# Graph net on one core: the scaling product issued behind the finished block, the column stored behind the rows, index work ahead of the degree counts

## The chip, the core and the metric

The kernel runs on one core of one Trainium2 chip. TensorE (PE) does the matrix products, VectorE (DVE) and ScalarE (ACT) the element-wise work, GpSimd (POOL) issues the indirect DMAs that gather rows, and SyncE (SP) issues the other DMAs. The metric is the device time of the program in microseconds; the time of a kernel is the median of several executions.

## What is computed

`x` has 6250 rows (nodes) of 512 float32; `src` and `dst` are 100000 edges, sorted by `dst`. Cut to what matters, the reference is:

```python
def _cheb_norm(src, dst, n):
    deg = segment_sum(ones, src, num_segments=n)
    dinv = where(deg > 0, rsqrt(maximum(deg, 1.0)), 0.0)
    return -dinv[src] * dinv[dst]

def _cheb_conv(x, src, dst, norm, W0, W1, b):
    tx1 = segment_sum(x[src] * norm[:, None], dst, num_segments=n)
    return x @ W0 + tx1 @ W1 + b

h = maximum(layernorm(x), 0.0)
h = _cheb_conv(h, src, dst, norm, W1_0, W1_1, b1)
h = _layer_norm(h, gamma, beta)
h = where(h >= 0, h, 0.01 * h)
return x + _cheb_conv(h, src, dst, norm, W2_0, W2_1, b2)
```

Each of the two layers gathers one row of 512 floats for every edge, sums the gathered rows by target node, and multiplies rows and sums by two 512 x 512 matrices.

## The kernel before, in words

**Tiling.** Nodes are cut into 49 blocks of 128 (`NB`), edges into 782 chunks of 128 (`NC`). One indirect DMA of POOL gathers one chunk, 128 rows, into one slot of the ring `places` (55 slots, `R`). Three chunks are a unit, four units a group; there are 66 groups (`NS`). Group 0 holds chunks 0 to 2, group 1 chunks 3 to 14, and so on by twelves; group 4 is chunks 39 to 50, group 64 759 to 770, and the last, group 65, 771 to 781. Gather number n writes slot n modulo 55, so that gather 94 overwrites chunk 39, the first of group 4.

**Tables.** Layer 0 gathers from `tab[0]`: rows of relu(layernorm(x)), whose column 512 holds the node's `dinv`. Layer 1 gathers from `tab[1]`, rows of the first layer's output, already scaled. While `tab[0]` is being made, the first 64 chunks (`RAW`) are gathered from `x` itself (`gather_raw`, L232 to L234) and scaled afterwards, when `look_up` (L475 to L495) has found the factors of their rows: it makes one-hot products on PE (L469, L484), multiplies them on DVE (L472, L487, L490, L493) and lets ACT scale four slots (L495). Its tile `both` (L489) lies in the buffer named `g`, of which there is one; `finish` uses that buffer too.

**Prologue.** `x` comes into the ring by blocks. DVE and PE count the degrees with one-hot matrices (L284 to L314; `lo` and `hi` at L300, 25 turns, into which ACT's row statistics and the row stores L272 are mixed). `load_rest` (L193) loads the rest of `x`, then, at its numbers 3 and 4, the two weights of the first layer and four bias rows. Behind the counts come `dinv`, the column store L340 (column 512 of the first 31 blocks of `tab[0]`, each piece four bytes), the last blocks' rows, and the index work L356 to L389: target indices transposed (L368, L371, L372), the units' first nodes (L375, L376), `node_of` (L388).

**The loop over groups** (L768 on) does for each group g: `gather_to` (issue the gathers up to a ring ahead), in layer 0 `look_up`, then `turn` for each block that is due (all its groups have been summed): `place` (L620 to L630: DVE's comparison `there` L628 and PE's product L630 bring the unit sums to the block's rows), and `own` (L507 to L516, the block's own rows turned by PE). Then `choose` (L549, the selection matrices `sel`), in layer 0 `scale` (L588 to L598: DVE multiplies `sel` by the gathered column 512, so it waits for the gathers of the group), `sums` (L601 to L618: PE's product L609 of `sel` and gathered rows), and `dense` for the due blocks (L684 to L698: PE's transposes L688, DVE's copy L690, 16 PE products L526), which calls `finish`. `finish` (L633 to L669) adds the bias (L647), takes the statistics (L650, L651), normalizes (L655 to L657), makes the scaled row (L660, L661), stores it to `tab[1]` (L664), makes the unscaled row in `g` (L666, L667) and stores it to `h_tab` (L669).

**The layer boundary.** For blocks 46 to 48 the part with the block's own rows is made early (`EARLY`, `early` L537). At group 64 the due blocks' `dense` comes ahead of the sums, and `gather_ahead` (L444 to L447) issues 18 gathers of layer 1, which need only the rows of `tab[1]` up to block 46; the next gathers (L437) need all of them.

**What sets the order.** On PE, POOL and SP instructions go in the order in which the code issues them (`manual_schedule`; in the prologue on SP alone). On DVE and ACT a scheduler puts them in order; `issue_after` gives it an instruction behind which another must be placed. Each engine works through its order one by one, and a waiting instruction holds what stands behind it.

Of the kernel before, what the change touches and what calls it, by code (L numbers as in the profile page):

```python
# [8 lines left out]
F32 = mybir.dt.float32  # L9
# [32 lines left out]
def gnn_kernel(  # L42
# [194 lines left out]

    gather_raw(0, RE)


    rs_all, nb_all = ln[:, 0, :], ln[:, 1, :]
    nm_all = ep.tile([P, NB], F32, name="nm_all")
# [41 lines left out]
    with tc.tile_pool(name="deg", bufs=1) as dp, tc.tile_pool(name="onehot", bufs=2) as ohp, tc.tile_pool(  # L284
        name="deg_ps", bufs=1, space=bass.MemoryType.PSUM
    ) as dps:
        s_lo = dp.tile([EP, EJ], BF, name="s_lo")
        s_hi = dp.tile([EP, EJ], BF, name="s_hi")
        half_i = dp.tile([EP, EJ], I32, name="half_i")
        nc.vector.tensor_single_scalar(half_i, src_i, LO - 1, op=OP.bitwise_and)  # L290
        nc.vector.tensor_copy(s_lo, half_i)
        half_i = dp.tile([EP, EJ], I32, name="half_i")
        nc.vector.tensor_single_scalar(half_i, src_i, 6, op=OP.arith_shift_right)
        nc.vector.tensor_copy(s_hi, half_i)
        both_ps = dps.tile([P, 2 * HI], F32, name="both_ps")
        for g in range(EJ // (2 * GJ)):
            hot = []
            for s, n, name in ((s_lo, LO, "lo"), (s_hi, HI, "hi")):
                t = ohp.tile([EP, GJ, n, 2], BF, name=name)
                nc.vector.tensor_tensor(  # L300
                    t, s[:, g * 2 * GJ : (g + 1) * 2 * GJ].rearrange("p (j s) -> p j s", s=2)[:, :, None, :]
                    .to_broadcast([EP, GJ, n, 2]),
                    iota_g[:EP, None, :n, :].to_broadcast([EP, GJ, n, 2]), op=OP.is_equal)
                hot.append(t.rearrange("p j n s -> p j (n s)"))
            k = turns.get(g)
            if k is not None:
                spread(*some[k])
                make_table(*some[k])
                load_rest(k - 1)
                if k + 2 < len(some):  # L310
                    stats(*some[k + 2])
            for j in range(GJ):
                nc.tensor.matmul(both_ps, hot[0][:, j, :], hot[1][:, j, :], start=(g == 0 and j == 0),
                                 stop=(g == EJ // (2 * GJ) - 1 and j == GJ - 1))  # L314
        nc.vector.tensor_copy(both, both_ps.rearrange("p (b t s) -> p b t s", t=2, s=2))
# [20 lines left out]
        nc.vector.tensor_scalar_mul(ndinv, dinv, -1.0)  # L336
        nc.vector.tensor_scalar_mul(sdinv, dinv, SLOPE)

    early = NB - LAST
    nc.sync.dma_start(tab[0][: early * P, D : D + 1].rearrange("(i p) o -> p i o", p=P), dinv[:, :early, None])  # L340
    for i0, n in others:
        cols = slice(i0, i0 + n)
        st = ep.tile([P, 7, 6], F32, name="st")
        mv = ep.tile([P, 7, 2], F32, name="mv")
        for j in range(n):
            nc.vector.bn_stats(st[:, j, :], places[:, RE + i0 + j, :D])
            nc.vector.bn_aggr(mv[:, j, :], st[:, j, :])
        nc.scalar.activation(rs_all[:, cols], mv[:, :n, 1], AF.Sqrt, bias=eps)
        nc.vector.reciprocal(rs_all[:, cols], rs_all[:, cols])
        nc.vector.scalar_tensor_tensor(nb_all[:, cols], mv[:, :n, 0], -1.0, rs_all[:, cols], op0=OP.mult, op1=OP.mult)  # L350
        nc.vector.tensor_copy(places[:, RE + i0 : RE + i0 + n, D : D + 1], dinv[:, cols, None])
        make_table(i0, n)
    nc.vector.tensor_mul(sc[:, 0, :], rs_all, dinv)
    nc.vector.tensor_mul(sc[:, 1, :], nb_all, dinv)

    low = ep.tile([P, P], I32, name="low")  # L356
    nc.vector.tensor_single_scalar(low, chunks[0][:, 0, :], P - 1, op=OP.bitwise_and)
    nc.vector.tensor_copy(src_lo, low)
    nc.vector.tensor_copy(pick, ident)


    nc.vector.memset(dlx[:, 0:1], 0.0)
    nc.vector.memset(dlx[:, 1 + NC :], float(N))
    with tc.tile_pool(name="turn", bufs=1) as wp, tc.tile_pool(
        name="turn_ps", bufs=1, space=bass.MemoryType.PSUM
    ) as wps:
        f = wp.tile([P, NG, P], F32, name="f")
        nc.vector.tensor_scalar_add(f, chunks[1], 1.0)  # L368
        dl_ps = wps.tile([P, NG * P], F32, name="dl_ps")
        for g in range(NG):  # L370
            nc.tensor.transpose(dl_ps[:, g * P : (g + 1) * P], f[:, g, :], ident)  # L371
        nc.scalar.activation(dlx[:, 1 : 1 + NC], dl_ps[:, :NC], AF.Copy)  # L372
        last = ident[:, P - 1 : P]
        first_ps = nodes_ps[:, : NQ * NS + 1]
        nc.tensor.matmul(first_ps, last.to_broadcast([P, P]), dlx[:, 0 : STEP * NQ * NS + 1 : STEP], start=True, stop=True)  # L375
        nc.vector.tensor_copy(first, first_ps)  # L376
        row_ps = wps.tile([P, NS], F32, name="row_ps")
        for q in range(NQ):
            for g, n in ((0, 1), (1, NS - 1)):
                at = STEP * (unit[g] + q)  # L380
                nc.tensor.matmul(row_ps[q * Q : (q + 1) * Q, g : g + n], last.to_broadcast([P, Q]),
                                 dlx[:, at : at + STEP * NQ * (n - 1) + 1 : STEP * NQ], start=True, stop=True)
        p_i = ep.tile([P, 1], I32, name="p_i")
        p_j = ep.tile([P, 1], F32, name="p_j")
        nc.vector.tensor_copy(p_i, p_id)
        nc.vector.tensor_single_scalar(p_i, p_i, Q - 1, op=OP.bitwise_and)
        nc.vector.tensor_copy(p_j, p_i)
        nc.vector.tensor_scalar(node_of, row_ps, p_j, None, op0=OP.add)  # L388
        nc.vector.tensor_scalar_mul(minus, last, -1.0)  # L389

    edges.close()
    unseen = const.tile([1, 1], I32, name="unseen")
# [9 lines left out]
def usual_path(tc, have):  # L402
    nc = tc.nc
    (x, out, tab, h_tab, ndinv, sidx, dlx, iota_r, w_sb, W2_1, W2_0, w_late, ident, eps, ones, first, nodes_ps, node_of, minus,
     unsorted, ln, dinv, sdinv, bias1, bias2, gam, bet, unseen, unit, N, E, D, NB, NC, NU, NS, KD, rows, places, R,
     sc, pick, src_lo, src_hi, eidx, e_src, zero_row, p_id) = (
        have[n] for n in ("x out tab h_tab ndinv sidx dlx iota_r w_sb W2_1 W2_0 w_late ident eps ones first nodes_ps node_of "
                          "minus unsorted ln dinv sdinv bias1 bias2 gam bet unseen unit N E D NB NC NU NS KD rows places "
                          "R sc pick src_lo src_hi eidx e_src zero_row p_id").split())
# [11 lines left out]
    with ExitStack() as es:  # L421
        pool = es.enter_context(tc.tile_pool(name="main", bufs=2))
        psum = es.enter_context(tc.tile_pool(name="main_ps", bufs=2, space=bass.MemoryType.PSUM))
        es.enter_context(tc.manual_schedule(engines={PE, POOL, SP}))
        is_lo, found, looked, gathered = [], 0, 0, R
        own_h, own_x, agg, placed, started, pre, late = {}, {}, {}, {}, {}, {}, {}
        SHIFTED = D - D % P
        lidx = pool.tile([P, NC - SHIFTED], I32, name="lidx", bufs=1)
# [46 lines left out]
        def look_up(tag):  # L475
# [7 lines left out]
            for j in range(4):  # L483
# [2 lines left out]
            is_hi = pool.tile([P, KD, P], F32, name="aT", bufs=1)[:, :, :NB]  # L486
            nc.vector.tensor_tensor(is_hi, src_hi[:, at : at + 4, None].to_broadcast([P, 4, NB]),  # L487
                                    iota_r[:, None, :NB].to_broadcast([P, 4, NB]), op=OP.is_equal)
            both = pool.tile([P, D], F32, name="g", bufs=1)[:, : 8 * NB].rearrange("p (j k b) -> p j k b", j=4, k=2)  # L489
            nc.vector.tensor_tensor(both, at_lo[:, :, : 2 * NB].rearrange("p j (k b) -> p j k b", k=2),  # L490
                                    is_hi[:, :, None, :].to_broadcast([P, 4, 2, NB]), op=OP.mult)
            ac = pool.tile([P, 4, 2], F32, name="ac", bufs=4)
# [127 lines left out]
        def place(i, some):  # L620
# [4 lines left out]
            for g in some:  # L625
                m = Q * (unit[g + 1] - unit[g])
                there = pool.tile([P, P], F32, name="there", bufs=3)
                nc.vector.tensor_scalar(there[:m, :r], iota_r[:m, :r], node_of[:m, g : g + 1], -(1.0 + i * P),  # L628
                                        op0=OP.subtract, op1=OP.is_equal)
                nc.tensor.matmul(placed[i][:r], there[:m, :r], agg[g][:m, :], start=(g == inside[i][0]),  # L630
                                 stop=(g == inside[i][-1]))

        def finish(layer, i, v):  # L633
# [23 lines left out]
            nc.vector.scalar_tensor_tensor(v, v, rs[:r], bet[:r], op0=OP.mult, op1=OP.add)  # L657

            t = late[i] if i in late else pool.tile([P, D], F32, name="t")
            nc.scalar.activation(t[:r], v, AF.Copy, scale=sdinv[:r, i : i + 1])  # L660
# [3 lines left out]
                nc.sync.dma_start(tab[1][at + lo : at + hi, :], t[lo:hi])  # L664
# [81 lines left out]
        high = pool.tile([P, RAW], I32, name="high", bufs=1)  # L746
        nc.vector.tensor_single_scalar(high, sidx[:, :RAW], 7, op=OP.arith_shift_right)
        nc.vector.tensor_copy(src_hi, high)
        find("ps")
        find("ps")  # L750
        for i in range(AHEAD):
            load(0, i)
        for k in range(2):
            look_up("u_ps")
            find("ps")

        for layer in range(2):
# [5 lines left out]
            for g in range(NS):  # L763
# [380 lines left out]
```

## Time and profile before

| quantity | value |
|---|---|
| median of 3 runs | 2081.95 us |
| fastest and slowest run | 2077.32 and 2086.94 us |
| profiled execution, its own time | 2079.41 us |
| span of the profile | 2077.0 us |
| PE, DVE, ACT, POOL busy | 81%, 34%, 21%, 73% of the span |

The profile is of one execution. Its span runs from the first to the last recorded instruction; what lies between span and time is outside the record. A busy share is a mean over the whole span, so the places where an engine waits have to be looked for one by one. PE's matrix products of float32 are recorded in two passes each: x24 stands for 12 products. In the timeline a row gives start, duration, engine, line, the operation's tiles, and in brackets the idle time ahead of it and what ended it. In the chain of waits each row is a step of the chain that ended last. Where a window is shown, the columns are the busy times of PE, weight load, DVE, ACT and POOL with their counts, the granted PE clock as a share, the DMA share and GB/s.

### The profile page before, as it was taken

How to read it: one execution, taken by the hardware profiler on the slowest of the kernel's cores; microseconds unless marked ns; L12 is line 12 of the kernel's file. 1: busy time of each engine (PE TensorE's matmuls, PEld its weight loads, DVE VectorE, ACT ScalarE, POOL GpSimd, SP SyncE). 2: the span in 40 equal slices, each digit the busy share in tenths (PEclk: the TensorE clock that was granted, in tenths of full speed). 3: DMA queues.
4: the chain of work that ended last, by engine and by line, in shares of the span. 5: the costliest groups of instructions: out<-in, count | busy, mean ns of one | idle time of the engine just before them, and what ended most of it. 6: DMA issues, size and time to landing. Idle time of an engine off the chain costs nothing.

```text
span 2077.0 us, 19822 instructions
## 1 busy us (share of the span) xinstructions
PE 1680.6 (81%) x6806; PEld 677.0 (33%) x6806; DVE 696.7 (34%) x1496; ACT 442.0 (21%) x789; POOL 1509.3 (73%) x1578
## 2 busy tenths in 40 slices
PE   4577977886869398779789888898888878888987
PEld 4443432332323143223333323233323223332332
DVE  7964433333344254324353121221212112111221
ACT  8883212222212122222121010110101011010110
POOL 5756777777777777777747777777777777777773
PEclk9778989999879799989999899999999999999999
DMA  9997888888888888888857788887888788888874
GB/s 334 375 288 220 271 262 247 263 261 246 262 281 266 231 277 262 249 263 255 259 171 239 244 247 249 255 256 241 255 240 255 240 256 255 250 246 251 274 237 145
DMA packets 189982, 528.49 MB, mean 254 GB/s; under 512 B 34610, under 2 KB 36172, under 8 KB 189872
## 3 DMA queue, kind: packets, MB, share of 16 engines
q0 software_dynamic: 125120, 415.98, 67.3%
q1 hardware_dynamic: 64752, 111.16, 14.8%
q8 instruction: 55, 0.90, 0.2%
q14 instruction: 55, 0.45, 0.1%
HBM read 475.35 MB, written 51.66 MB: 254 GB/s over the span
## 4 chain that ended last, share of the span: by engine, by line
PE 32%; DMA 29%; POOL 16%; issue 14%; DVE 7%; ACT 2%; DVEq 0%; POOLq 0%; SPq 0%; ACTq 0%
DMA places<-tab,sidx 22%; POOL places L437 16%; PE u_ps L526 13%; PE ps L609 8%; PE an_ps L630 6%; DMA places<-tab,lidx 6%; PE hT_ps L688 1%; DVE lo L300 1%; DVE hi L300 1%; PE hT_ps L514 1%; ACT an L681 1%; PE hT_ps L484 1%; DVE st L650 1%; PE hT_ps L581 0%; DVE sel L598 0%
## 5 line engine op out<-in xcount | busy, mean ns | idle before, releaser
L437 POOL DMA_INDIRECT places<-tab,sidx x1212 | 1149.7, 949 | 376.5 <-issue 268.5
L609 PE MATMUL ps<-places,sel 128*32 128x512 f32 x3128 | 495.6, 642 | 126.5 <-DMA places<-tab,sidx 86.4
L437 POOL DMA_INDIRECT places<-tab,lidx x270 | 255.6, 947 | 82.3 <-issue 63.1
L630 PE MATMUL an_ps<-agg,there 128*128 128x512 f32 (+1 forms) x580 | 277.1, 611 | 17.4 <-ACT agg L618 17.4
L609 PEld LDWEIGHTS ps<-places,sel 128*32 128x32 f32 x3128 | 100.6, 113 | 489.3 <-issue 195.3
L526 PE MATMUL u_ps<-w,aT 128*128 128x512 f32 (+1 forms) x392 | 181.3, 606 | 33.7 <-DVE aT L690 33.7
L565 DVE TENSOR_TENSOR sel<-dlx,nodes_ps 128x384 f32<-128x384 f32 (+3 forms) x134 | 72.1, 539 | 403.3 <-PE ps L609 403.3
L526 PE MATMUL u_ps<-w,hT 128*128 128x512 f32 (+1 forms) x392 | 197.6, 652 | 5.4 <-ACT hT L516 5.4
L618 ACT ACTIVATE agg<-ps 128x512 f32<-128x512 f32 (+1 forms) x132 | 78.5, 594 | 538.5 <-PE ps L609 516.9
L526 PE MATMUL u_ps<-places,hT 128*128 128x512 f32 (+1 forms) x392 | 185.0, 616 | 2.2 <-ACT hT L516 2.2
L526 PE MATMUL u_ps<-places,aT 128*128 128x512 f32 (+1 forms) x392 | 178.2, 598 | 2.3 <-DVE aT L690 2.3
L598 DVE TENSOR_TENSOR sel<-sel,places 128x384 f32<-128x384 f32 (+11 forms) x73 | 35.3, 486 | 380.5 <-DMA places<-tab,sidx 359.4
L688 PE MATMUL hT_ps<-ident,an 128*128 128x128 f32 x392 | 71.8, 311 | 106.0 <-ACT an L681 105.4
L630 PEld LDWEIGHTS an_ps<-agg,there 128*128 128x128 f32 (+1 forms) x580 | 104.8, 196 | 120.9 <-issue 90.3
L641 DVE TENSOR_TENSOR u_ps<-u_ps,bias 128x512 f32<-128x512 f32 x46 | 32.2, 700 | 283.0 <-PE u_ps L526 283.0
L516 ACT ACTIVATE hT<-hT_ps 128x512 f32<-128x512 f32 (+1 forms) x98 | 58.0, 592 | 291.8 <-PE hT_ps L514 291.0
L526 PEld LDWEIGHTS u_ps<-w,aT 128*128 128x128 f32 (+1 forms) x392 | 74.0, 193 | 134.0 <-issue 85.9
L234 POOL DMA_INDIRECT places<-in_x_dram,sidx x55 | 74.9, 1361 | 54.7 <-DMA tab<-places 15.5
L628 DVE TENSOR_SCALAR there<-iota_r,node_of 128x128 f32<-128x128 f32 (+1 forms) x290 | 86.3, 301 | 83.0 <-PE an_ps L630 82.7
L688 PEld LDWEIGHTS hT_ps<-ident,an 128*128 128x128 f32 x392 | 46.1, 154 | 197.6 <-ACT an L681 139.0
L526 PEld LDWEIGHTS u_ps<-w,hT 128*128 128x128 f32 (+1 forms) x392 | 79.3, 213 | 89.8 <-issue 83.7
L526 PEld LDWEIGHTS u_ps<-places,aT 128*128 128x128 f32 (+1 forms) x392 | 74.6, 191 | 96.5 <-issue 93.6
(159 smaller groups left out, 1265.3 us busy)
## 6 DMA issues: line engine op xcount, KB each, us to landing
places<-tab,sidx POOLq DMA_INDIRECT x1212, 3.8
h_tab<-g SPq DMA_DIRECT2D x48, 256.0 KB
xt<-in_x_dram SPq DMA_DIRECT2D x48, 256.0 KB
out_dram<-t SPq DMA_DIRECT2D x48, 256.0 KB
tab<-t SPq DMA_DIRECT2D x47, 256.0 KB
h<-in_x_dram SPq DMA_DIRECT2D x46, 256.0 KB
h<-h_tab SPq DMA_DIRECT2D x46, 256.0 KB
tab<-places SPq DMA_DIRECT2D x22, 528.0 KB
```

Of the source, the lines that this page charges most:

```text
L234: nc.gpsimd.indirect_dma_start(out=places[:, t, :D], out_offset=None, in_=x, in_offset=bass.IndirectOffsetOnAxis(ap=sidx[:, t : t + 1], ax ...
L300: nc.vector.tensor_tensor(t, s[:, g * 2 * GJ : (g + 1) * 2 * GJ].rearrange("p (j s) -> p j s", s=2)[:, :, None, :] .to_broadcast([EP, GJ, ...
L437: nc.gpsimd.indirect_dma_start(out=places[:, t % R, :] if own_scale else zr(layer, t), out_offset=None, in_=x if layer == 0 and t < RAW el ...
L516: nc.scalar.activation(hT[:, :, :r], ps[:, :, :r], AF.Copy)
L526: nc.tensor.matmul(u_ps[:r], hT[:, kc, :r], w[:, kc, :], start=(start and kc == 0), stop=(stop and kc == KD - 1))
L565: nc.vector.tensor_tensor(sel[:, q : q + k, :w, :], of, node[:, q : q + k, None, :].to_broadcast([P, k, w, Q]), op=OP.is_equal)
L598: nc.vector.tensor_tensor(v, v, places[:, lo % R : lo % R + hi - lo, D : D + 1].to_broadcast([P, hi - lo, Q]), op=OP.mult)
L609: nc.tensor.matmul(ps[q * Q : (q + 1) * Q, :], sel[:, q, s, :], zr(layer, chunk[q][s]), start=(s == 0), stop=(s == len(chunk[q]) - 1 and ( ...
L618: nc.scalar.activation(agg[g][: n * Q], ps[: n * Q], AF.Copy)
L628: nc.vector.tensor_scalar(there[:m, :r], iota_r[:m, :r], node_of[:m, g : g + 1], -(1.0 + i * P), op0=OP.subtract, op1=OP.is_equal)
L630: nc.tensor.matmul(placed[i][:r], there[:m, :r], agg[g][:m, :], start=(g == inside[i][0]), stop=(g == inside[i][-1]))
L688: nc.tensor.transpose(ps[:, kc, :r], an[:r, kc * P : (kc + 1) * P], ident[:r, :r])
```

## The change

Three stretches of code change their place, one tile its buffer, and one product its place in DVE's order. No operation is added or left out.

1. The index work (L356 to L389) and the high bits of the source indices (`high`, `src_hi`, L746 to L748) are written ahead of the row statistics and the degree counts.
2. The column store L340 stands behind the row stores of the last blocks instead of ahead of them.
3. The weights and biases (`load_rest(3)`, `load_rest(4)`) are loaded behind the first two loads of `usual_path` instead of in turns of the degree counts.
4. The tile `both` of `look_up` lies in the buffers named `an` (two) instead of `g` (one).
5. In layer 0 `scale` is issued behind the last comparison `there` and behind the last finished block: behind its L657, and from block 45 on behind its last step L667.

```diff
+        high = ep.tile([P, RAW], I32, name="high")
+        nc.vector.tensor_single_scalar(high, sidx[:, :RAW], 7, op=OP.arith_shift_right)
+        nc.vector.tensor_copy(src_hi, high)
...
-                load_rest(k - 1)
+                if k < 4:
+                    load_rest(k - 1)
...
-    early = NB - LAST
-    nc.sync.dma_start(tab[0][: early * P, D : D + 1].rearrange("(i p) o -> p i o", p=P), dinv[:, :early, None])
     for i0, n in others:
...
         make_table(i0, n)
+    early = NB - LAST
+    nc.sync.dma_start(tab[0][: early * P, D : D + 1].rearrange("(i p) o -> p i o", p=P), dinv[:, :early, None])
...
+        behind = {}
...
-            both = pool.tile([P, D], F32, name="g", bufs=1)[:, : 8 * NB].rearrange("p (j k b) -> p j k b", j=4, k=2)
+            both = pool.tile([P, D], F32, name="an")[:, : 8 * NB].rearrange("p (j k b) -> p j k b", j=4, k=2)
...
-                nc.vector.tensor_scalar(there[:m, :r], iota_r[:m, :r], node_of[:m, g : g + 1], -(1.0 + i * P),
-                                        op0=OP.subtract, op1=OP.is_equal)
+                behind[1] = nc.vector.tensor_scalar(there[:m, :r], iota_r[:m, :r], node_of[:m, g : g + 1],
+                                                    -(1.0 + i * P), op0=OP.subtract, op1=OP.is_equal)
...
-            nc.vector.scalar_tensor_tensor(v, v, rs[:r], bet[:r], op0=OP.mult, op1=OP.add)
+            behind[0] = nc.vector.scalar_tensor_tensor(v, v, rs[:r], bet[:r], op0=OP.mult, op1=OP.add)
...
-            nc.vector.tensor_tensor(g[:r], v, g[:r], op=OP.max)
+            end = nc.vector.tensor_tensor(g[:r], v, g[:r], op=OP.max)
+            if i >= NB - 4:
+                behind[0] = end
...
         for i in range(AHEAD):
             load(0, i)
+        load_rest(3)
+        load_rest(4)
...
                 if layer == 0:
-                    scale(sel, chunk)
+                    with ExitStack() as order:
+                        for ins in behind.values():
+                            order.enter_context(tc.issue_after(ins.ins))
+                        scale(sel, chunk)
```

The stretch of the index work is written word for word as it was, only further up.

More of the change, by code (lines that the diff above doesn't have):

```diff
@@ L238, in gnn_kernel @@
     gather_raw(0, RE)
+    low = ep.tile([P, P], I32, name="low")
+    nc.vector.tensor_single_scalar(low, chunks[0][:, 0, :], P - 1, op=OP.bitwise_and)
+    nc.vector.tensor_copy(src_lo, low)
+    nc.vector.tensor_copy(pick, ident)
+    nc.vector.memset(dlx[:, 0:1], 0.0)
+    nc.vector.memset(dlx[:, 1 + NC :], float(N))
+    with tc.tile_pool(name="turn", bufs=1) as wp, tc.tile_pool(
+        name="turn_ps", bufs=1, space=bass.MemoryType.PSUM
+    ) as wps:
+        f = wp.tile([P, NG, P], F32, name="f")
+        nc.vector.tensor_scalar_add(f, chunks[1], 1.0)
+        dl_ps = wps.tile([P, NG * P], F32, name="dl_ps")
+        for g in range(NG):
+            nc.tensor.transpose(dl_ps[:, g * P : (g + 1) * P], f[:, g, :], ident)
+        nc.scalar.activation(dlx[:, 1 : 1 + NC], dl_ps[:, :NC], AF.Copy)
+        last = ident[:, P - 1 : P]
+        first_ps = nodes_ps[:, : NQ * NS + 1]
+        nc.tensor.matmul(first_ps, last.to_broadcast([P, P]), dlx[:, 0 : STEP * NQ * NS + 1 : STEP], start=True, stop=True)
+        nc.vector.tensor_copy(first, first_ps)
+        row_ps = wps.tile([P, NS], F32, name="row_ps")
+        for q in range(NQ):
+            for g, n in ((0, 1), (1, NS - 1)):
+                at = STEP * (unit[g] + q)
+                nc.tensor.matmul(row_ps[q * Q : (q + 1) * Q, g : g + n], last.to_broadcast([P, Q]),
+                                 dlx[:, at : at + STEP * NQ * (n - 1) + 1 : STEP * NQ], start=True, stop=True)
+        p_i = ep.tile([P, 1], I32, name="p_i")
+        p_j = ep.tile([P, 1], F32, name="p_j")
+        nc.vector.tensor_copy(p_i, p_id)
+        nc.vector.tensor_single_scalar(p_i, p_i, Q - 1, op=OP.bitwise_and)
+        nc.vector.tensor_copy(p_j, p_i)
+        nc.vector.tensor_scalar(node_of, row_ps, p_j, None, op0=OP.add)
+        nc.vector.tensor_scalar_mul(minus, last, -1.0)
+        high = ep.tile([P, RAW], I32, name="high")
+        nc.vector.tensor_single_scalar(high, sidx[:, :RAW], 7, op=OP.arith_shift_right)
+        nc.vector.tensor_copy(src_hi, high)
     rs_all, nb_all = ln[:, 0, :], ln[:, 1, :]
@@ L352, in gnn_kernel @@
         make_table(i0, n)
+    early = NB - LAST
+    nc.sync.dma_start(tab[0][: early * P, D : D + 1].rearrange("(i p) o -> p i o", p=P), dinv[:, :early, None])
     nc.vector.tensor_mul(sc[:, 0, :], rs_all, dinv)
     nc.vector.tensor_mul(sc[:, 1, :], nb_all, dinv)
[L356 to L389, printed above, removed]
     edges.close()
@@ L405, in usual_path @@
      unsorted, ln, dinv, sdinv, bias1, bias2, gam, bet, unseen, unit, N, E, D, NB, NC, NU, NS, KD, rows, places, R,
-     sc, pick, src_lo, src_hi, eidx, e_src, zero_row, p_id) = (
+     load_rest, sc, pick, src_lo, src_hi, eidx, e_src, zero_row, p_id) = (
         have[n] for n in ("x out tab h_tab ndinv sidx dlx iota_r w_sb W2_1 W2_0 w_late ident eps ones first nodes_ps node_of "
                           "minus unsorted ln dinv sdinv bias1 bias2 gam bet unseen unit N E D NB NC NU NS KD rows places "
-                          "R sc pick src_lo src_hi eidx e_src zero_row p_id").split())
+                          "R load_rest sc pick src_lo src_hi eidx e_src zero_row p_id").split())
     AHEAD = 2
@@ L744, in check @@
             nc.vector.tensor_single_scalar(unseen, ok[:, 0:1], 0.0, op=OP.is_gt)
-        high = pool.tile([P, RAW], I32, name="high", bufs=1)
-        nc.vector.tensor_single_scalar(high, sidx[:, :RAW], 7, op=OP.arith_shift_right)
-        nc.vector.tensor_copy(src_hi, high)
         find("ps")
```

## The prediction

> **What bounds the kernel now.** I read the page first, then the waits of POOL, then POOL's timeline. The page names the costliest group: the single-chunk gathers.
>
> ```profile
> span 2077.0 us, 19822 instructions
> L437 POOL DMA_INDIRECT places<-tab,sidx x1212 | 1149.7, 949 | 376.5 <-issue 268.5
> ...
> POOL places L437 <- issue: 331.8, 1089, 0.3
> POOL places L234 <- DMA tab<-places: 15.5, 4, 7.5
> ```
>
> A gather takes 0.95 and is followed by 0.30 of issue: 1.25 us each, 15.0 for a group of 12. Beside these pauses of 0.3 the waits (engine and line, who was waited for, us in total, times, longest) hold only a few long ones, and the timeline (start, duration, in brackets the idle time ahead and what ended it) gives their places.
>
> ```profile
> 121.58 0.95 POOL L234 DMA_INDIRECT places<-in_x_dram,sidx  x1 [7.96 <-ACT agg L618]
> ...
> 145.34 0.94 POOL L437 DMA_INDIRECT places<-tab,sidx  x1 [0.30 <-DMA places<-in_x_dram,sidx]
> 187.04 0.94 POOL L437 DMA_INDIRECT places<-tab,sidx  x1 [4.50 <-ACT places L495]
> 1049.23 0.95 POOL L437 DMA_INDIRECT places<-tab,sidx  x1 [0.30 <-issue]
> 1070.53 0.94 POOL L447 DMA_INDIRECT places<-tab,eidx  x1 [20.35 <-DMA tab<-t]
> 1096.05 0.94 POOL L437 DMA_INDIRECT places<-tab,sidx  x1 [3.29 <-DMA tab<-pre]
> ```
>
> From 187.04 to 1049.23 POOL issues without a gap (gathers 94 to 781: 862.2 / 687 = 1.255 each), and again from 1096.05 on. So three things set the time: when gather 94 goes, how long POOL stands between 1049.23 and 1096.05, and a fixed rest. An edit that shortens PE or DVE anywhere else buys nothing. Faster and slower mean by more than 0.5% here, 10.4 us, about what a measurement of this kernel can tell from no change.
>
> **Gather 94: the `both` tile.** Gather 94 overwrites slot 39, the first chunk of group 4, so it waits for that group's products. What held these is in the chain of waits:
>
> ```profile
> 167.67 0.70 DVE u_ps L647
> 168.37 0.26 DVE aT L487
> ...
> 170.87 0.77 DVE u_ps L657
> ...
> 174.52 5.46 DMA h_tab<-g
> 180.07 0.58 DVE g L490
> 181.81 3.52 PE an_ps L630 x6
> 185.32 2.71 PE ps L609 x24
> ...
> 196.40 2.71 PE ps L609 x24
> ```
>
> The look-up at L490 writes into the one buffer `g`, which the first finished block has filled and its store of 256 KB is still reading: 5.46 us, behind L667 of that block. In `an`, with two buffers, neither stands in the way. The earliest L490 can go is behind its operand L487, at 168.6 (gain 11.4); the latest, if DVE still sets it behind the whole of the finished block, 174.5 (gain 5.6). DVE takes look-up and block by turns there, so I put L490 just ahead of L657, at 170.8: 9.3 sooner. PE's transposes, L630 and L609 follow as they did. Gather 94 came 1.7 behind the start of L609 and would go at 187.04 - 9.3 = 177.7. POOL waited 4.50 for it, so it was ready at 182.5; the 4.8 that it lacks must come from its stalls further up (next part). Late next would be gather 106 on group 5: L609 at 196.40 - 9.3 = 187.1, plus 1.7 is 188.8, against POOL's 177.7 + 15.0 = 192.7. Hidden, with 3.9 to spare; what it costs beyond that is one for one.
>
> **Column and weights.** The column store and the load of two weights move on SP's queue.
>
> ```profile
> 110.04 0.37 SPq L340 DMA_DIRECT2D tab<-dinv  x1
> ...
> w<-in_L_gnn_W_dram SPq DMA_DIRECT2D x2, 1024.0 KB
> ```
>
> The first row is SP's timeline, the second the list of DMA issues. The column (128 x 31 pieces of four bytes, 15.5 KB) went out at 110.04 ahead of ten row stores, and the gather at 121.58 waited for a row store queued behind it; so column and rows together took at most 11.5. With the column last, the raw gathers no longer stand behind it: the 7.5 and 8.0 shrink, which is where POOL gets its head start. In exchange the first gather of the table, 145.34 before, must wait for the column. Issued behind the row stores at about 113 to 119 and landing within the same 11.5, it is there by 131. POOL would reach that gather at 145.34 - 15.5 = 129.8 at best; but gather 94 lies 30 x 1.25 = 37.5 further and is not wanted before 177.7, so the column may land as late as 140. Cost nothing; if it lands later than 140, each microsecond counts.
>
> The two weights and four biases (2 x 1024 KB, and 4 tiles of 128 x 512 floats, 3.1 MB) come behind the row stores and two loads. At the 249 GB/s of the row of 140 to 160 below that is 12.3 us, so they land at about 146. The first user is the dense product at 160.76 (`w`), then L647 at 167.67 (`bias`). Hidden by 14 us; without that cover the whole chain above would slide.
>
> ```profile
> 140.00:160.00 20.00, 11.49 (x46) 4.33 (x46) 3.13 (x10) 11.46 (x17) 15.13 (x17) 0.66 0.84 249
> 160.76 6.88 PE u_ps L526 x16
> ```
>
> **Index work.** It only changes its place; DVE starts the degree counts at 12.38 and sets the pace of the prologue.
>
> ```profile
> 12.38 0.58 DVE L290 TENSOR_SCALAR half_i<-src_i 125x800 int32<-125x800 int32 x1 [4.66 <-PE fT L229]
> 97.00 0.61 DVE L368 TENSOR_SCALAR f<-dst_c 128x896 f32<-128x896 int32 x1
> 97.75 1.73 PE L371 MATMUL dl_ps<-ident,f 128*128 128x128 f32 x7 [6.25 <-DVE ln L349]
> 104.09 0.21 DVE L354 TENSOR_TENSOR sc<-ln,dinv 128x49 f32<-128x49 f32 x1
> 105.66 0.44 DVE L376 COPY first<-nodes_ps 128x265 f32<-128x265 f32 x1 [1.36 <-PE nodes_ps L375]
> 107.17 1.41 DVE L472 TENSOR_SCALAR xt<-ps,p_id 128x512 f32<-128x512 f32 x2
> ```
>
> Ahead of the loop: `f` 0.61, PE's transposes 1.73 that must read `f` before `half_i` takes its memory, `first` 0.44, and a short sum like it: 3.1 later at the loop's end. Behind it, what DVE does between `sc` (104.30) and L472 (107.17) is gone, 2.9. Net +0.2, which gives 9.3 - 0.2 = 9.1; I take 9.0. Bounds: -1.1 (`f` and PE's 1.73 hidden in the 4.66 that DVE waits there anyway, the rest kept) to +3.1 (nothing saved behind).
>
> **The layer in between: scale behind the block.** Before, DVE runs the product `sel` times gathered column for group g+1 ahead of the block that PE has just finished, and stands until the gathers land, with the block behind it.
>
> ```profile
> 1038.20 0.53 DVE L598 TENSOR_TENSOR sel<-sel,places 128x352 f32<-128x352 f32 x1 [9.32 <-DMA places<-tab,sidx]
> 1053.26 0.26 DVE L598 TENSOR_TENSOR sel<-sel,places 128x96 f32<-128x96 f32 x1 [1.67 <-DMA places<-tab,sidx]
> 1057.63 5.26 PE L526 MATMUL u_ps<-w,aT 128*128 128x512 f32 x8 [0.78 <-DVE aT L690]
> 1067.76 0.32 SPq L664 DMA_DIRECT2D tab<-t  x1
> 1070.57 3.70 PE L526 MATMUL u_ps<-w,aT 128*128 128x512 f32 x8 [0.78 <-DVE aT L690]
> 1075.06 4.57 PE L609 MATMUL ps<-places,sel 128*32 128x512 f32 x22
> 1091.51 0.73 SPq L664 DMA_DIRECT2D tab<-pre  x2
> ```
>
> In the changed order the block goes first (L647 to L657, from 167.67 to 171.64 above, 4.0), and scale (0.53) follows. This makes a serial loop: products of a group, transposes, dense product, block, scale, next products. In the chain's rows:
>
> ```profile
> 204.99 0.59 PE hT_ps L688 x4
> 205.58 6.87 PE u_ps L526 x16
> 212.45 0.44 PE hT_ps L514 x4
> 212.89 2.58 PE an_ps L630 x6
> ...
> 300.00:400.00 100.00, 80.77 (x305) 32.66 (x306) 37.71 (x86) 21.92 (x39) 75.75 (x80) 0.88 0.85 256
> ```
>
> 2.71 (L609) + 0.59 + 6.87 + 4.0 + 0.5 = 14.7, with L514 and L630 (3.0) inside DVE's 4.5. At most 49 of the 66 groups have a block, the others need about 2.71 + 3.0, 6 at the most: 12.5 on the mean against POOL's 15.0. So within the layer nothing changes; the cover is 2.5 a group.
>
> At its end the blocks no longer stand behind gathers of a group that PE hasn't reached. The dense product of block 46 (1057.63) moves up by one group of gathers and the 0.9 of hand-over, to 1041.7; at 3.70 instead of 5.26 its store leaves at 1041.7 + 10.1 - 1.6 = 1050.2, and POOL goes on with the gathers ahead at 1052.9, 17.6 sooner. But these are 18: 22.5 us, over at 1075.4, and then POOL waits for blocks 47 and 48. There the new order costs: scale(64) stands behind block 46 complete, products of 64 at 1052.3, dense 47 to 1063.8, block 47 complete at 1070.0 (6.2 for a block, which took 6.85 above with the look-up between), scale(65), products of 65 at 1070.7 instead of 1075.06. The last store follows 16.45 later, at 1087.1, and POOL at 1091.6: 4.4 sooner. The floor is a loss of 6 (loop three groups late), the ceiling both waits, 23.6; I take 3.5, near the working, with 0.9 for the lag that the loop may carry there.
>
> **Sum.** 2079.4 of the profiled execution (span 2077.0 and 2.4 around it) - 9.0 - 3.5 = 2066.9. That execution lies 2.5 below the median, so 2069.4 in its measure: 2069.
>
> **Rivals.** A, the clock takes the boundary: the row of 1057.63 shows 5.26 for what the next block does in 3.70, after PE had stood while the last gathers held DVE. For: the serial end makes more such gaps. Against: within the layer PE idles only 1 us a turn. Two blocks at 1.6 eat the 3.5 of it: 2073. [...]
>
> B, the column or the weights land late: if the table's first gather is held to 150, gather 94 stands at 187 again and the 9.0 is gone: 2078. For: 3.1 MB on the same queue behind the column. Against: they are queued behind it, not ahead.
>
> C, slower: the serial loop exceeds POOL's 15.0. It decides where a turn with a block takes 3.4 more than 14.7 (2.5 x 66 / 49). Each microsecond beyond that costs 49/66 x 60 groups, 45 us: with 0.5 beyond it 2069 + 22 = 2091, with 1.5 2136. For: PE was busy 80.77 of 100, so little of it can hide the block. Against: at the clock of 0.88 in that row PE's 10.2 of the loop would have to become 13.6, a clock of 0.66.
>
> D, more: products of 65 follow dense 47 at 1063.8 without the block between them, another 6.9, and L490 goes behind L487, another 2.1: 2060. For: all gathers have landed by 1053.3. Against: from block 45 on scale waits for the block's last step, L667.
>
> **Chances.** Forecast 0.55, A 0.12, B 0.09, C 0.14, D 0.10. Below 2071.5 (0.5% under 2081.95) counts as faster: 0.8 of the forecast, a third of A and all of D, 0.58. Slower is C and a little of B, 0.15; the rest 0.27. The likeliest case alone is 2063 to 2077 (gather 94 by 7 to 11, boundary -5 to +3). The range takes in D below and, above, B and the cheapest of C: 2057 to 2090.
>
> **What would show it.** Right: gather 94 at 177 to 178; no store between L667 and L490 in the chain; POOL's wait ahead of L447 about 2 to 3 instead of 20.4, and about 16 ahead of L437 on the last stores; stalls at L234 smaller; DVE waiting for PE, not for gathers, ahead of L598. Wrong: POOL gaps of over 0.3 inside 200 to 1040 (C); gather 94 waiting for a column or weight (B); the first gather of layer 1 no sooner against gather 781 (A).

## The result and the profile after

Twenty runs of each: 2079.78 us after (2074.64 to 2085.52) against 2084.38 before (2077.32 to 2086.95), a ratio of 0.9978 with a 95% interval of 0.9969 to 0.9987. That is 4.6 us faster, within 0.5% and so no change by the bound of the prediction; 12.9 were forecast (2081.95 to 2069).

The page of the changed kernel and POOL's timeline answer to the rows of before; its lines from L430 on have moved by five and from L669 on by seven, so L437 is L442 and L447 is L452 (every kernel below has its own line numbers):

```profile
span 2078.3 us, 19910 instructions
...
133.14 0.95 POOL L442 DMA_INDIRECT places<-tab,sidx  x1 [1.92 <-ACT places L500]
176.63 0.95 POOL L442 DMA_INDIRECT places<-tab,sidx  x1 [3.67 <-ACT places L500]
1042.22 0.95 POOL L442 DMA_INDIRECT places<-tab,sidx  x1 [0.30 <-issue]
1054.57 0.95 POOL L452 DMA_INDIRECT places<-tab,eidx  x1 [11.41 <-DMA tab<-t]
1096.21 0.95 POOL L442 DMA_INDIRECT places<-tab,sidx  x1 [19.38 <-DMA tab<-pre]
```

Cut at gather 94, gather 781 and the first gather that needs the whole second table, the spans compare so: 187.0 / 862.2 / 46.8 / 981.0 before, 176.6 / 865.6 / 54.0 / 982.1 after. The prologue gave 10.4; the layer boundary took 7.2 back, and the layer 3.4. The whole prologue gain is gone at 1096: 1096.05 before, 1096.21 after. The two profiled executions don't show the 4.6 of the medians: that of before lay 5.0 below the median of its twenty runs, that of after 1.2 above, and by the spans after is even 1.3 longer. Such scatter can be seen in the last stretch, from the first gather that needs the whole second table to the end, where no kernel of this document differs in its code: it took 977.6 to 982.1 in the ten profiles of the table below. So single microseconds of one profile decide nothing.

What took the gain of the prologue back stands in PE's timeline of the boundary:

```profile
1028.20 2.78 PE L614 MATMUL ps<-places,sel 128*32 128x512 f32 x24 [0.95 <-DVE sel L603]
...
1043.23 3.70 PE L531 MATMUL u_ps<-w,aT 128*128 128x512 f32 x8 [0.78 <-DVE aT L697]
1053.62 5.31 PE L614 MATMUL ps<-places,sel 128*32 128x512 f32 x24 [6.69 <-DVE sel L603]
...
1074.26 6.97 PE L614 MATMUL ps<-places,sel 128*32 128x512 f32 x22 [5.80 <-DVE sel L603]
```

The products of groups 64 and 65 wait 6.69 and 5.80 for the scaling product, which waits for a whole block, though the last gather (issued at 1042.22) had landed at 1046.7, before either wait began. Behind the gaps they take 5.31 and 6.97; in before's timeline those of 65 took 4.57 and those of 64 this:

```profile
1062.82 2.78 PE L609 MATMUL ps<-places,sel 128*32 128x512 f32 x24
```

What lengthens them is PE's clock. In the windows of these two products the granted clock was 0.52 and 0.64:

```profile
1053.62:1058.93 5.31, 5.31 (x25) 1.06 (x25) 0.04 (x1) 0.00 (x0) 3.44 (x4) 0.52 0.48 152
1074.26:1081.23 6.97, 6.97 (x22) 1.52 (x22) 0.12 (x1) 0.00 (x0) 1.96 (x3) 0.64 0.63 208
```

### The profile page after: what moved, and what is told of

Read it like the earlier page. It is cut to its first block, busy times and chain, and to the rows that moved or that the text cites. A ratio compares the mean times of both kernels' runs of the same rounds, so it can differ in the third digit from the quotient of the medians.

```text
span 2078.3 us, 19910 instructions
## 1 busy us (share of the span) xinstructions
PE 1690.1 (81%) x6806; PEld 677.0 (33%) x6806; DVE 707.3 (34%) x1496; ACT 448.1 (22%) x789; POOL 1515.3 (73%) x1578
## 4 chain that ended last, share of the span: by engine, by line
DMA 35%; PE 31%; POOL 13%; issue 11%; DVE 6%; ACT 2%; SPq 1%; DVEq 0%; POOLq 0%; ACTq 0%
DMA places<-tab,sidx 26%; POOL places L442 13%; PE u_ps L531 13%; PE ps L614 10%; DMA places<-tab,lidx 6%; PE an_ps L635 4%; DMA h<-in_x_dram 2%; PE hT_ps L695 1%; DVE hi L338 1%; DVE lo L338 1%; PE hT_ps L519 1%; DVE sel L603 1%; ACT places L500 1%; SPq L506 1%; DMA w<-in_L_gnn_W_dram 1%
## 5 line engine op out<-in xcount | busy, mean ns | idle before, releaser
L442 POOL DMA_INDIRECT places<-tab,sidx x1212 | 1154.3, 952 | 395.9 <-issue 257.3
L614 PE MATMUL ps<-places,sel 128*32 128x512 f32 x3128 | 527.1, 680 | 218.3 <-DVE sel L603 92.4
L442 POOL DMA_INDIRECT places<-tab,lidx x270 | 256.2, 949 | 82.3 <-issue 59.2
L614 PEld LDWEIGHTS ps<-places,sel 128*32 128x32 f32 x3128 | 106.6, 118 | 605.9 <-DMA places<-tab,sidx 187.4
L531 PE MATMUL u_ps<-places,hT 128*128 128x512 f32 (+1 forms) x392 | 182.1, 608 | 2.2 <-ACT hT L521 2.2
L531 PE MATMUL u_ps<-w,hT 128*128 128x512 f32 (+1 forms) x392 | 181.1, 606 | 2.2 <-ACT hT L521 2.2
L646 DVE TENSOR_TENSOR u_ps<-u_ps,bias 128x512 f32<-128x512 f32 x46 | 32.2, 700 | 280.2 <-PE u_ps L531 280.2
L652 DVE TENSOR_TENSOR u_ps<-u_ps,bias 128x512 f32<-128x512 f32 x46 | 32.2, 700 | 279.4 <-PE u_ps L531 279.4
L531 PEld LDWEIGHTS u_ps<-places,hT 128*128 128x128 f32 (+1 forms) x392 | 73.0, 197 | 76.7 <-issue 73.8
L531 PEld LDWEIGHTS u_ps<-w,hT 128*128 128x128 f32 (+1 forms) x392 | 72.4, 195 | 76.0 <-issue 73.2
L688 ACT ACTIVATE an<-an_ps,ndinv 128x512 f32<-128x512 f32 (+1 forms) x98 | 67.1, 685 | 138.1 <-PE an_ps L635 138.1
```

The costliest lines, as they stand in the source:

```text
L442: nc.gpsimd.indirect_dma_start(out=places[:, t % R, :] if own_scale else zr(layer, t), out_offset=None, in_=x if layer == 0 and t < RAW el ...
L531: nc.tensor.matmul(u_ps[:r], hT[:, kc, :r], w[:, kc, :], start=(start and kc == 0), stop=(stop and kc == KD - 1))
L614: nc.tensor.matmul(ps[q * Q : (q + 1) * Q, :], sel[:, q, s, :], zr(layer, chunk[q][s]), start=(s == 0), stop=(s == len(chunk[q]) - 1 and ( ...
L646: nc.vector.tensor_add(v, v, bias2[:r])
L688: nc.scalar.activation(an[:r], placed.pop(i)[:r], AF.Copy, scale=ndinv[:r, i : i + 1])
```

## The experiments

Each kernel ran beside runs of before on its own chip; a ratio counts against those. Two of the sets fell on chips on which before itself takes 2501 and 2503 us; they are told apart below. On the others before took 2076 to 2084. The columns are: time of gather 94, gather 94 to 781, 781 to the first gather that needs the whole second table, and PE's lag at group 63 (start of the copy `agg` of its sums less the issue of its last gather, 758), all from one profile each.

| kernel | 94 | 94 to 781 | boundary | lag | ratio (95%) |
|---|---|---|---|---|---|
| before | 187.0 | 862.2 | 46.8 | 24.4 | |
| after | 176.6 | 865.6 | 54.0 | 17.7 | 0.9978 (0.9969 to 0.9987) |
| y1 scale only | 188.8 | 864.5 | 57.9 | 21.6 | 1.0032 (1.0019 to 1.0044) |
| z2 all but scale | 174.2 | 863.2 | 46.5 | 24.3 | 0.9952 (0.9938 to 0.9965) |
| z3 tile only | 182.1 | 862.6 | 48.6 | 24.4 | 0.9970 (0.9959 to 0.9981) |
| z7 queue only | 184.6 | 862.7 | 47.1 | 24.5 | 0.9986 (0.9977 to 0.9995) |
| z9 L657 throughout | 175.7 | 864.9 | 45.7 | 17.2 | 0.9957 (0.9943 to 0.9970) |
| x4 shift later | 175.1 | 864.6 | 47.8 | 11.5 | 0.9963 (0.9949 to 0.9976) |
| x5 scale behind the copy at the end | 175.2 | 864.6 | 35.9 | 15.6 | 0.9922 (0.9908 to 0.9936) |
| x6 x4 and x5 | 176.7 | 865.1 | 31.1 | 9.4 | 0.9900 (0.9885 to 0.9915) |

**The scaling product alone, and everything but it.** y1 is before with edit 5 of the change, z2 the changed kernel without it:

```diff
...
                 if layer == 0:
-                    scale(sel, chunk)
+                    with ExitStack() as order:
+                        for ins in behind.values():
+                            order.enter_context(tc.issue_after(ins.ins))
+                        scale(sel, chunk)
```

> Before, with only the scaling product put behind the finished block, once more, for a chip on which before runs at about 2084 us. Theory: as there, gather 94 at 187, stretch from gather 781 to the first gather that needs the whole second table about 54 instead of 46.8; ratio about 1.003. Where before takes 2500 us instead, the ring is empty less often and the serial loop shows in POOL's waits inside the layer: ratio 1.024.

> The changed kernel without the edit of the scaling product. Theory (prologue and boundary are independent): gather 94 at 175 to 177, stretch from gather 781 to the first gather that needs the whole second table 47; ratio 0.995 where before takes about 2080 us. Rival (the earlier prologue lengthens the boundary by itself): stretch 54, ratio 0.998.

Measured: y1 stretches the boundary to 57.9 with gather 94 where it was, and is slower by 0.32%; z2 keeps 46.5 and is faster by 0.48%. The rival of both, that the earlier prologue lengthens the boundary, falls. The edit of the scaling product is the loss, the other edits are the gain, and the two ratios multiply to 0.9984, near the change's 0.9978; these are measured times, and don't rest on single profiles.

**Which edit brings gather 94 forward.** z3 is before with the one line of the tile, z7 before with the moves of `load_rest(3)`, `load_rest(4)` and the column store:

```diff
-            both = pool.tile([P, D], F32, name="g", bufs=1)[:, : 8 * NB].rearrange("p (j k b) -> p j k b", j=4, k=2)
+            both = pool.tile([P, D], F32, name="an")[:, : 8 * NB].rearrange("p (j k b) -> p j k b", j=4, k=2)
```

```diff
-                load_rest(k - 1)
+                if k < 4:
+                    load_rest(k - 1)
...
             load(0, i)
+        load_rest(3)
+        load_rest(4)
...
-    early = NB - LAST
-    nc.sync.dma_start(tab[0][: early * P, D : D + 1].rearrange("(i p) o -> p i o", p=P), dinv[:, :early, None])
     for i0, n in others:
...
         make_table(i0, n)
+    early = NB - LAST
+    nc.sync.dma_start(tab[0][: early * P, D : D + 1].rearrange("(i p) o -> p i o", p=P), dinv[:, :early, None])
```

> Before, with only the tile both in the buffers an. Theory (two conditions, PE's products and POOL's own readiness): gather 94 at 182.5 and without a wait, ratio 0.998 where before takes about 2080 us. Rival (the tile is all of it): 177, ratio 0.995.

> Before, with only the moves on SP's queue. Theory: first gather of the table at 130 to 134, gather 94 still at about 187 behind a wait of some 14, ratio 1.000 where before takes about 2080 us. Rival (queue brings PE's work forward): 180 or sooner, ratio 0.997 or less.

POOL's timeline at gather 94, z3 first, then z7:

```profile
182.06 0.95 POOL L437 DMA_INDIRECT places<-tab,sidx  x1 [0.30 <-ACT places L495]
```

```profile
131.81 0.95 POOL L438 DMA_INDIRECT places<-tab,sidx  x1 [0.30 <-issue]
...
184.61 0.95 POOL L438 DMA_INDIRECT places<-tab,sidx  x1 [12.67 <-ACT an L682]
```

With the tile alone POOL is the late one: it comes to gather 94 at 182.06 and needn't wait. With the queue alone POOL has its head start (131.81 instead of 145.34) and spends it waiting 12.67. So there are two conditions, and the later sets the time of gather 94: singly the edits give 5.0 and 2.4, together, with the index work, 12.8 in z2. z7 missed its expected 187 by 2.4, hardly more than the scatter of the profiles (187.0 and 188.8 in before and y1, 174.2 to 176.7 in the six kernels with all the edits of the prologue). The run times don't show that the edits need each other: 0.30% and 0.14% singly come near the 0.48% of z2, within the intervals.

**The index work alone** ran only on one of the chips of 2503 us:

```diff
+    low = ep.tile([P, P], I32, name="low")
+    nc.vector.tensor_single_scalar(low, chunks[0][:, 0, :], P - 1, op=OP.bitwise_and)
...
+        high = ep.tile([P, RAW], I32, name="high")
...
     rs_all, nb_all = ln[:, 0, :], ln[:, 1, :]
```

> Before, with only the index work ahead of the degree counts. Theory: the last turn of the degree counts ends 2 to 4 us later, the first look-up (L472) starts within 1 us of 107.2, gather 94 within 1 us of 187; ratio 1.000. Rival (the work is not hidden ahead of the counts): gather 94 at 189 to 191, ratio 1.001 to 1.002.

Measured 1.0006 (0.9972 to 1.0041): no effect that can be told, and too wide to tell the 0.1% of the rival. Its gather 94 went at 232.3, which says nothing of the expected 187, since before has no profile on such a chip.

**PE's lag.** In the changed kernel's timeline DVE stands 39 us in the middle of the layer, in `shift`, whose L466 overwrites indices that gathers still read; the scheduler had put it at group 40 though the code calls it at group 50. (L461, with 30.5, did so in before.)

```profile
705.82 0.43 DVE L466 CAST sidx<-xt 128x512 int32<-128x512 f32 x1 [39.12 <-DMA places<-tab,sidx]
...
709.15 6.10 PE L531 MATMUL u_ps<-w,aT 128*128 128x512 f32 x8 [36.77 <-DVE aT L697]
```

PE's lag behind the gathers (measured as in the table) rose to 56.6 at group 40, in before to 53.9. Before had worked it off at group 46, to 21.7; after still had 31.9 at group 50. x4 pins `shift` behind group 50's block:

```diff
-                    shift(0, SHIFTED)
-                    shift(SHIFTED, NC)
+                    with ExitStack() as order:
+                        for ins in behind.values():
+                            order.enter_context(tc.issue_after(ins.ins))
+                        shift(0, SHIFTED)
+                        shift(SHIFTED, NC)
```

> The changed kernel with shift (the index rewrite that DVE runs at group 40, where L466 waits 39 us for gathers that still read the old indices) issued behind the block of group 50 instead. Theory (PE is late at the boundary because the serial loop works off this hole at only 2 us a group): no wait at L466, PE's lag at group 63 falls from 17.7 to about 10, dense 46 and its store come 8 us sooner, wait ahead of the first early gather 11.4 to about 4, stretch 54 to 46, ratio about 0.994. Rival (the lag comes from the three early blocks of groups 55 to 59 alone): stretch 52 to 54, ratio 0.998 as for the change.

L466 no longer waits, the lag fell to 11.5 and the boundary to 47.8, 6.2 less than after; 8 had been expected. The ratio is 0.15% better than that of after, 3 us, about half of this, and short of the expected 0.994; but the two are from different chips.

**The end of the layer.** x5 puts only the last two scaling products behind DVE's copy `aT` of the dense product, z9 takes the stronger condition (behind the block's last step) away from the last blocks:

```diff
-            nc.vector.tensor_copy(aT[:, :, :r], ps[:, :, :r])
+            copied = nc.vector.tensor_copy(aT[:, :, :r], ps[:, :, :r])
...
             finish(layer, i, u_ps)
+            if NB - 4 < i < NB - 1:
+                behind[0] = copied
```

```diff
-            if i >= NB - 4:
-                behind[0] = end
```

> The changed kernel with the scaling products of groups 64 and 65 issued behind DVE's copy aT of the dense product instead of behind the whole finished block. Theory (PE stands 6.7 and 5.8 us for them, and pays 2.6 and 2.4 us more at a lower clock): PE's gaps ahead of these two products go, they take 2.8 and 4.6, last store 17 us sooner, the gather waiting for it too, stretch 54 to about 37, ratio about 0.990. Rival (the blocks' own chain on DVE sets the last store, the gaps are covered): stretch 50 or more, ratio 0.996 or more.

> The changed kernel with scale behind L662 (the changed kernel's number of L657) for the last blocks too, not behind the block's last step. Theory (PE's gaps ahead of the last two products set the end): gaps 6.7 and 5.8 shrink by 2.5 to 3 each, stretch 54 to 48 or 49, ratio 0.995 where before takes about 2080 us. Rival (scale in the middle of the block delays the block's store by as much): stretch 53 or 54, ratio 0.998.

PE's timeline of the same products, x5, then z9:

```profile
1042.41 2.78 PE L614 MATMUL ps<-places,sel 128*32 128x512 f32 x24
...
1054.65 4.57 PE L614 MATMUL ps<-places,sel 128*32 128x512 f32 x22
```

```profile
1048.29 4.16 PE L614 MATMUL ps<-places,sel 128*32 128x512 f32 x24 [3.81 <-DVE sel L603]
...
1065.17 4.57 PE L614 MATMUL ps<-places,sel 128*32 128x512 f32 x22 [2.92 <-DVE sel L603]
...
1073.64 5.26 PE L531 MATMUL u_ps<-w,aT 128*106 128x512 f32 x8 [0.69 <-DVE aT L695]
```

In x5 the gaps are gone, the products take 2.78 and 4.57 again, at a granted clock of 1.00, and the boundary falls by 18.1, as expected. On the same chip x5's median is 2058.34, 9.6 under the 2067.97 of x4, which has the gaps; the expected ratio of 0.990 was missed by 0.2%. z9 went further than expected (45.7 instead of 48 to 49): its products take 1.2 and 2.4 less than those of after, of which block 48's dense product gives 1.6 back (5.26 instead of 3.68). So the condition on the last blocks alone costs 8.3 at the boundary. Without it the scaling product's new place is worth nothing either way: z9 and z2, which leaves that edit out, ran on one chip and took 2067.74 and 2067.73.

**Both.** x6 joins x4 and x5.

> Both: shift behind group 50 and the last two scaling products behind the copy. Theory: the two gains add, stretch from gather 781 to the first gather that needs the whole second table about 28 to 30 (18 gathers ahead take 22.5 of it), ratio about 0.986. Rival (POOL's own early gathers bound it): stretch 37, ratio 0.990 as with the tail alone.

The boundary is 31.1, where the two gains in full would give 29.7. One product of PE covers the shortfall of 1.4: the dense product of block 48, whose store the next gathers wait for, took 5.38, where x5 shows 3.68.

```profile
1058.88 5.38 PE L531 MATMUL u_ps<-w,aT 128*106 128x512 f32 x8 [0.69 <-DVE aT L697]
```

POOL's own 18 early gathers take 22.5 of the boundary, but do not bound it: 4.74 and 3.11 of waiting are left. With 0.9900 against before x6 beats both kernels, and its median of 2055.18 is 3.2 under that of x5 on the same chip; the expected 0.986 was missed by 0.4%.

**On chips of 2500 us** x1 is the kernel of y1:

> Before, with only the scaling product put behind the finished block. Theory (the new order itself lengthens the layer boundary): gather 94 stays at 187, the stretch from gather 781 to the first gather that needs all of the second table grows from 46.8 us to about 54, products of groups 64 and 65 come behind PE gaps of 6 to 7 us and take 5.3 and 7.0 instead of 2.7 and 4.6; ratio about 1.003. Rival (the boundary is longer in the changed kernel only because its gathers run ahead of PE after the shorter prologue): stretch 47, ratio 1.000.

It measured 1.0241 (1.0194 to 1.0289), 54 us slower. x2 and y2 are z2's kernel, x3 and y3 z3's, x7 and y7 z7's:

> The changed kernel without the edit of the scaling product. Theory: gather 94 at 177, stretch from gather 781 to the second table's last rows back at about 47; 10 us under before, ratio about 0.995. Rival (the earlier prologue causes the longer boundary): gather 94 at 177, stretch 54, ratio 0.998 as for the whole change.

> The changed kernel without the edit of the scaling product, again for a chip on which before takes about 2080 us. Theory (prologue and boundary add): gather 94 at 176 to 177, stretch from gather 781 to the first gather that needs the whole second table 47, ratio about 0.995. Rival (the earlier prologue lengthens the boundary by itself): stretch 54, ratio 0.998.

These two gave 0.9967 (0.9936 to 0.9998) and 0.9949 (0.9914 to 0.9983).

> Before, with only the tile both in the buffers an. Theory (two conditions for gather 94: PE's products and POOL's own readiness): PE is ready at 177 but POOL, with its two stalls of over 7 us kept, only at 182.5; gather 94 at 182.5, ratio about 0.998. Rival (the tile is all of it): gather 94 at 177, ratio 0.995. Second rival (DVE puts the look-up behind the block anyway): gather 94 at 185 or later, ratio 0.999 to 1.000.

> Before, with only the tile both in the buffers an, again for such a chip. Theory: PE's products of group 4 are ready for gather 94 at 177, POOL with its two long stalls only at 182.5; gather 94 at 182.5 without a wait, ratio 0.998. Rival (the tile is all of it): 177, ratio 0.995.

These gave 0.9957 (0.9926 to 0.9988) and 0.9970 (0.9938 to 1.0002).

> Before, with only the moves on SP's queue (weights, biases and the column store). Theory: POOL's stalls ahead of the last raw gathers shrink, the first gather of the table goes at 130 to 134 instead of 145.3, but gather 94 still waits for PE's products of group 4 until about 187, with a wait of 14 instead of 4.5; ratio 1.000. Rival (the earlier row stores bring PE's work forward too): gather 94 at 180 or sooner, ratio 0.997 or less.

> Before, with only the moves on SP's queue, again for such a chip. Theory: first gather of the table at 130 to 134, gather 94 still at about 187 behind a wait of 14, ratio 1.000. Rival (queue brings PE's work forward): 180 or sooner, ratio 0.997 or less.

These gave 0.9988 (0.9958 to 1.0017) and 0.9991 (0.9965 to 1.0017). The expected times of gather 94 don't hold here: it went at 212.8 to 225.7 in these six, 225.6 in x1. z2's kernel is faster here too; of z3's the second interval, and of z7's both, take in no change. The scaling product is seven times as dear (54 us against 7.8). POOL's waits of x1 name it:

```profile
POOL places L438 <- PE ps L610: 212.2, 60, 13.4
```

POOL there waits for slots inside the layer: 212.2 us in all for these products, in the other six 125.5 to 182.0, while before, in its profile above, waits for them only within its pauses of 0.3. Gathers 94 to 781 took 1071.7 in x1 and 1014.1 to 1036.2 in the six, 35 to 58 less, so the 54 lie in the layer. The reading that fits is that PE's loop decides there, so that a longer loop shows at once; no run tests it by itself.

## Why the prediction was wrong

The measured 2079.8 lies inside the range of 2057 to 2090, but that is the width of the range: the likeliest case added two gains, and one of the two was a loss.

**The bound** was right: gathers 94 to 781 run without a gap in both kernels, and gather 94 and the boundary decide, but for 3.4 that came between them.

**Gather 94** was right in mechanism and size: 177.7 was forecast, 176.63 came. The chain of waits of the changed kernel shows L490 (now L495) between the steps of the block, with no store ahead of it:

```profile
168.67 0.70 DVE u_ps L652
169.72 0.43 issue
170.16 0.56 DVE an L495
```

L495 went at 170.16, where 170.8 had been taken. The head start through the queue is shown by z3 and z7: both edits are needed for it, as the prediction said. (It read the stall of 7.96 ahead of the gather at 121.58 as a wait for a row store; the row itself names ACT's copy `agg`. That this stall and the one of 7.34 hang on the queue is shown by z7, in which both are gone.) The index work delayed the end of the degree counts by 1.8 (3.1 forecast) and L472 began at 107.08 instead of 107.17. Column, weights and biases cost nothing: the table's first gather went at 133.14, inside the 140 allowed.

**The boundary** is where it failed: 3.5 to be gained, 7.2 lost. Taken from gather 781, the steps were forecast and came so:

| step | forecast | after |
|---|---|---|
| dense 46 | -7.5 | +1.0 |
| first early gather (L447) | +3.7 | +12.4 |
| products of 64 | +3.1 | +11.4 |
| products of 65 | +21.5 | +32.0 |
| last store | +37.9 | +50.9 |
| first gather that needs all | +42.4 | +54.0 |

The first error is the sentence "I take 3.5, near the working, with 0.9 for the lag that the loop may carry there": dense 46 came 8.5 behind the working. The working let PE follow the gathers at once, because 12.5 a group left a cover of 2.5. That cover was well sized (PE's lag falls from 57.1 at group 41 to 38.5 at group 49, 2.3 a group), but it was read as slack and not as the only means of catching up: the wait of L461 stood in the trace of before and was not looked for. Of the 8.5, x4 shows 6.2. The other 2.3 stay open; three early blocks come just ahead of the end (at groups 55, 57 and 59; the lag rises to 32.2 at group 56), but no run leaves them out.

The second error is the clock, rival A, which had been given 0.12: 2.5 at group 64 and 2.4 at group 65, behind gaps of 6.69 and 5.80. The forecast had these two waits in its own working (scale behind a whole block) and yet took the spacings of before, with products of 2.78 and 4.57, for what follows them. 8.5 and 4.9 make 13.4; of these the last store is 13.0 late, and the gather behind it 11.6, as it followed the store 1.4 sooner than forecast. A's price of 3.5 was too low. That the clock and not the product is the cause is shown by the granted clock, 0.52 and 0.64 in after's two products and 1.00 in x5's, which follow without a gap. The sign that the prediction named for A, the first gather of layer 1 no sooner, did not show: that gather depends on dense 46, ahead of both products.

**"Within the layer PE idles only 1 us a turn"** held for three groups of four. In the other 14, which have no block to place, PE waited 3.62 to 3.85 and their products took 4.2 to 5.4 instead of 2.78. With them four groups took 51.1 (207.88 to 258.98), 12.8 each instead of 12.5. The 2 us more from gather 94 to 781 come in all six kernels with the new order (864.5 to 865.6) and in none of the four without (862.2 to 863.2). In after they are not a pause: its pauses sum to 209.5, those of before to 209.3, while the gathers themselves take 656.1 instead of 652.9; why was not settled.

**Rival C** did not decide here; on the chips of 2500 us a loss of its kind came, 54 us inside the layer. **D** is, in its place, nearly what x5 made: the products of 65 following dense 47.

## What to carry to other kernels

A chain that is hidden with a small margin catches up only at that margin: look for the largest single stall ahead of the place where the chain ends, and count the groups left to work it off. Where an order is pinned to free one engine, pin it behind the last operand that is really needed (here the copy that PE waits for) and not behind the whole neighbour. Where two conditions hold one transfer, ask of each what the other still allows: here lifting one left POOL late, lifting the other left it waiting.

## What the hardware showed

The length of the last idle gap did not tell whether PE's clock was cut. In after, products ran at a granted clock of 0.52 and 0.64 behind gaps of 6.69 and 5.80, and in z9 at 0.65 behind 3.81 (4.16 instead of 2.78). But in x6 the products of one group ran at 1.00 behind a gap of 3.85, and the dense product of 5.38 shown above ran at 0.68, though PE's gaps in the 30 us ahead of it were 0.78 at most:

```profile
999.42 2.78 PE L614 MATMUL ps<-places,sel 128*32 128x512 f32 x24 [3.85 <-DVE sel L603]
```

In z9 the products behind 2.92 ran at 1.00, and the dense product 8.5 us later at 0.69. The Trainium skill has for this, in "TensorE: Matmul & The Clock Gate", section "HAM oscillation — how this bites in real kernels", the rule that PE should have no idle gaps of more than some 3.4 us. The gaps of 3.81 to 6.69 above agree with it, the rows of x6 do not: there a longer gap cost nothing, and a product was slowed behind gaps far shorter.

The same kernel took 2076 to 2084 us on some chips and 2501 to 2503 on others. The profiles taken on the others, of its variants, show 0.84 of the clock instead of 0.91 to 0.92 and 207 to 212 GB/s instead of 253 to 258; what sets the chips apart was not looked into.
